# Two-layer image attention: PSUM as four double pairs, keys and queries by pairs of strips, earlier value windows, half of the next image behind layer 0

## The chip, the core and the metric

One core of a Trainium2 chip runs the whole program. Its engines work side by side and meet through semaphores: TensorE (PE; its weight loads are shown as PEld) multiplies into PSUM, VectorE (DVE) and ScalarE (ACT) read PSUM and write SBUF, GpSimd (POOL) works in SBUF alone, and SyncE (SP) issues the DMAs. Each engine takes its own instructions in program order. The metric is the time of one execution on the device in microseconds (us), lower is better; the program runs once over a batch of 16 images.

## What is computed

Each image has 64 x 64 positions and 256 channels in fp32. Two layers follow each other, each a group norm, an attention and a residual add. Layer 0 is linear attention over the whole image, layer 1 is attention over a 7 x 7 neighbourhood with a learned positional term; both have 8 heads of 32 channels.

```python
x = x + L0(_gn(x));  x = x + L1(_gn(x))
# L0, per head: n = 4096 positions
q = softmax(q, over 32 channels) * 32**-0.5;  k = softmax(k, over n)
context = einsum('bhdn,bhen->bhde', k, v);  out = einsum('bhde,bhdn->bhen', context, q) @ w_out
# L1, per position and head: the 49 neighbours (zero padded)
scores = einsum('bhwnd,bhwndk->bhwnk', q, unfold(k, 7) + e)     # e: row and column embeddings
out = einsum('bhwndk,bhwnk->bhwnd', unfold(v, 7), softmax(scores))
```

## The kernel before

An image lies as two tiles of 128 channels x 4096 positions (`x[0]`, `x[1]`), cut into 8 strips of 512. The host has ordered the positions in column blocks: strips 1 to 7 are each 8 columns wide over all 64 rows, shifted by three from the padded grid's blocks; strip 0 holds the two edges (5 and 3 columns) and is moved in two pieces (`pieces`, L474). The main loop runs over the images `b`; one image goes through these stages, in program order on every engine:

1. **Layer 0** (`layer0`, L515). For each of 16 pairs of token blocks PE makes queries and keys (L531) into a two-bank PSUM tile, ACT takes the exponential, and PE adds up the context (L549). `xn[0]` and `xn[1]` hold the normalised image; after the last L531 nothing of this layer reads `xn[1]`. Then the output product (L642) runs in 4 x 2 blocks of 64 matmuls; DVE adds each block to `x` (L653, L656) and takes statistics (L465).
2. **Group statistics** for layer 1 (`group_steps`, L257): DVE aggregates, copies the means (L265), PE averages over groups (L268), DVE forms the variance, PE averages again (L277), POOL makes the reciprocal root (L281).
3. **Positions** (`positional_products` L692, `positional` L703): products of four pairs of strips into four PSUM banks, moved by DVE (pairs 0, 2) and ACT (pairs 1, 3). `fold_bias` (L670) and the `foldv` product (L1036) fold the group means into biases; `bvn` (L1039) is the value bias. `store_rings` (L714) writes the positional scores to DRAM in 16 DMAs.
4. **Values** (`values`, L734): eight strips in the order `KEYED = (2,3,4,5,6,7,1,0)`, 16 matmuls each, a bias add by DVE in two halves (L746), then a DMA to the padded value image `vpad` in DRAM (eight DMAs for strip 0). After the fourth strip `load_rings(0)` (L726) issues eight DMAs that bring positional scores and a mask into rows of `qq`.
5. For each half `hg` of the heads (0, 1): **keys and queries** (`keys_queries`, L760), then **attention** (`local_attention`, L807).

`keys_queries` makes all keys in four steps of two strips, then all queries in four steps. `banks` (L375) hands out PSUM in turn: double tile 0 (moved by DVE), double tile 1 (moved by ACT), single banks 0 and 1, single banks 2 and 3 (one bank by DVE, one by ACT). `evacuate` (L681) moves 32 rows x 512 positions at a time and adds the bias, one instruction for each head and strip (L684 on ACT, L686 on DVE). The last query step is held back by a `yield` until the first scores are issued.

`local_attention` first writes a mask value into both double tiles (L951), then works on four units of 16 columns, in the order `UNITS = (1,2,3,0)`. A unit has nine row chunks in five groups. For each chunk: scores (L834) into a double tile, an exponential on ACT (L843 for half 0, L846 for half 1), weighted values (L878) into single banks 0 and 1 (`outs`, opened by L885), an in-place add of overlapping rows on DVE (L863), and sums (L908) into banks 2 and 3 (`zs`). A step of the loop issues the scores of one group, the weighted values of the group before, the sums of the one before that. At a unit's end ACT copies `outs` (L970), DVE transposes `zs` (L915) and spreads the reciprocals (L921), POOL multiplies and adds to the image (L934, L942), and SP stores finished strips. `vw` holds the value windows of a unit: `load_window` (L795) issues four DMAs from `vpad`, two windows at a time are in SBUF.

Between groups, `between0` and `between1` put in work for the next image: in attention 0 the load of `x_next[1]` strip by strip during units 0 and 1 (L1074) and its statistics during units 2 and 3; in attention 1 the load of `x_next[0]` at the first group, its statistics at unit 1 (two strips per group), the three group-statistics steps at unit 2, groups 0 to 2, and the normalisation (L285) of two strips at unit 3, groups 1 and 2. The storage of `x_next[1]` is the present image's `xn[1]`. The order of PE, ACT, DVE and SP is exactly that of the program text; a DMA's issue on SP waits for what its data need and for the DMA eight issues earlier.

Of the kernel before, what the change touches and what calls it, by code (L numbers as in the profile page):

```python
# [19 lines left out]
P = 128  # L20
W = 64
# [21 lines left out]
ORDER = (4, 5, 6, 7, 0, 1, 2, 3)  # L43
EDGE = (5, 3)
# [44 lines left out]
class Net:  # L89
# [167 lines left out]
    def group_steps(self, stats, eps, small, psum, name, result):  # L257
# [5 lines left out]
        mean_c, var_c = mv[:, :, 0:1], mv[:, :, 1:2]  # L263
        rhs = small.tile([P, 2, 1], F32, tag="gn1", name=f"gn1{name}")
        nc.vector.tensor_copy(rhs, mean_c)  # L265
        yield
        pm = psum(f"pm{name}")
        nc.tensor.matmul(pm[:, 0:2], self.grp, rhs.rearrange("p a b -> p (a b)"), start=True, stop=True)  # L268
# [3 lines left out]
        nc.vector.tensor_tensor(d, rhs.rearrange("p a b -> p (a b)"), mean, ALU.subtract)  # L272
        nc.vector.tensor_tensor(d, d, d, ALU.mult)
        nc.vector.tensor_tensor(d, d, var_c.rearrange("p a b -> p (a b)"), ALU.add)
# [83 lines left out]
def attention_fast(tc, io, ok):  # L358
# [3 lines left out]
    with ExitStack() as ctx:  # L362
# [3 lines left out]
        double = [ps.tile([P, 2, 512], F32, tag=f"pd{i}", name=f"pd{i}") for i in range(2)]  # L366
        single = [ps.tile([P, 512], F32, tag=f"ps{i}", name=f"ps{i}") for i in range(4)]
        turn = [0, 0]

        def psum2():  # L370
            turn[0] += 1
            return double[turn[0] % 2]

        def banks():

            i = turn[1] % 4
            turn[1] += 1
            if i >= 2:
                return single[2 * i - 4 : 2 * i - 2], (0, 1)
            return [double[i][:, j] for j in range(2)], (i, i)  # L380
# [4 lines left out]
        def next_bank(name):  # L385

            return double[(turn[0] + 1) % 2][:, 0, 64:]
# [127 lines left out]
        def layer0(b, x, xn, mean, rstd, xtok, ready, midway=None):  # L515

            mu = None
            pc, other = single[:2], single[2:]
# [92 lines left out]
            for hg in range(2):  # L611
                for h in range(4):
                    rows = slice(HD * h, HD * h + HD)
                    nc.tensor.matmul(
                        double[h // 2][:, h % 2, hg * C : (hg + 1) * C],
                        ch[rows, hg * P : (hg + 1) * P],
                        n.wout_sb[rows, hg],
                        start=True,
                        stop=True,
                    )  # L620
# [3 lines left out]
            for h in range(2):  # L624
                nc.vector.tensor_copy(w4[:, h].rearrange("p g c -> p (g c)"), double[0][:, h])
            nc.scalar.copy(w4[:, 2:4].rearrange("p h g c -> p h (g c)"), double[1])
# [5 lines left out]
            for i in range(NS // 2):  # L632
# [3 lines left out]
                for co in range(2):  # L636
                    py = [double[a // 2][:, a % 2, : 2 * P] if co else single[a][:, : 2 * P] for a in range(4)]
                    for h in range(4):
                        for hg in range(2):
                            for a in range(4):  # L640
                                rows = slice(HD * a, HD * a + HD)
                                nc.tensor.matmul(  # L642
                                    py[a],
# [6 lines left out]
                    if co:  # L650
                        for a in (0, 2):
                            part = double[a // 2][:, :, : 2 * P].rearrange("p a (t n) -> p a t n", n=HD)
                            nc.vector.tensor_tensor(xv[:, a : a + 2], part, xv[:, a : a + 2], ALU.add)  # L653
                    else:
                        for a in range(4):
                            nc.vector.tensor_tensor(xv[:, a], py[a].rearrange("p (t n) -> p t n", n=HD), xv[:, a], ALU.add)  # L656
# [35 lines left out]
        def positional_products(i, x, pair):  # L692
            for k in range(2):
                for a in range(2):
                    nc.tensor.matmul(  # L695
                        single[i][64 * a : 64 * a + 64],
# [6 lines left out]
        def positional(i, pair):  # L703


            for a in range(2):
                for hg in range(2):
                    rows = slice(64 * a + 32 * hg, 64 * a + 32 * hg + 32)
                    image = placed(qq[32 * hg : 32 * hg + 32, 0], hg)
                    for _, _, m, w, view in pieces(pair[a]):  # L710
                        src = view(single[i][rows])
# [22 lines left out]
        def values(b, s, x):  # L734

            pv, _ = banks()
            v4 = work_tile(f"v4_{b}_{s}").rearrange("p (t c) -> p t c", c=C)
            for i in range(2):
                pi = pv[i].rearrange("p (t c) -> p t c", c=C)
                for t in range(2):  # L740
                    n0 = s * 512 + (2 * i + t) * P
                    for k in range(2):
                        nc.tensor.matmul(pi[:, t], x[k][:, n0 : n0 + P], wv[:, k], start=(k == 0), stop=(k == 1))  # L743
            for i in range(2):
                pi = pv[i].rearrange("p (t c) -> p t c", c=C)
                nc.vector.tensor_tensor(v4[:, 2 * i : 2 * i + 2], pi, bv.unsqueeze(1).to_broadcast([P, 2, C]), ALU.add)  # L746
# [13 lines left out]
        def keys_queries(b, hg, x):  # L760

            for what in range(2):
                for i in range(0, NS, 2):
                    if what and i == NS - 2:
                        yield
                    ps, engines = banks()
                    pair = KEYED[i : i + 2]
                    wgt = wq if what else wk
                    for a in range(2):
                        for k in range(2):  # L770
                            nc.tensor.matmul(  # L771
                                ps[a],
                                wgt[:, k, hg * P : (hg + 1) * P],
                                x[k][:, strip(pair[a])],
                                start=(k == 0),
                                stop=(k == 1),
                            )
                    for a in range(2):
                        for h in range(4):
                            rows = slice(h * HD, (h + 1) * HD)  # L780
                            d0 = 64 * (h % 2)
                            for u, p0, m, w, view in pieces(pair[a]):
                                src = view(ps[a][rows])
                                if what:
                                    dst = placed(qq[d0 : d0 + HD, h // 2], hg)[:, :, w : w + m]
                                else:
                                    dst = kaug[h // 2][d0 : d0 + HD, u, PAD : PAD + W, p0 : p0 + m]
                                dst = by_rows(dst, src)
                                if what and hg:

                                    order = "p r w -> p w r" if len(src.shape) == 3 else "p g r w -> p w g r"
                                    dst, src = dst.rearrange(order), src.rearrange(order)
                                evacuate(engines[a], dst, src, bias[rows, 2 * what + hg : 2 * what + hg + 1])
# [13 lines left out]
        def local_attention(b, hg, x, y, vw, queries, after_scores, between, stored):  # L807
# [3 lines left out]
            outs, zs = single[:2], single[2:]  # L811
# [98 lines left out]
            def finish(i, t, r, pvs):  # L910

                for k in range(2):


                    nc.vector.transpose(r[:, k], zs[k])  # L915
# [32 lines left out]
            for i in range(4):  # L948
                rows = slice(32 * i, 32 * i + 32)
                to = double[i // 2][:, i % 2]  # L950
# [3 lines left out]
            for step in range(len(groups) + 4):  # L954
# [8 lines left out]
                if held:  # L963
# [3 lines left out]
                    if g == 4:  # L967
                        rs[i] = [tail.tile([P, 2, 512], F32, tag=f"tail{k}", name=f"r{b}_{hg}_{i}_{k}") for k in range(2)]
                        for j in range(2):
                            nc.scalar.copy(rs[i][1][:, j], outs[j])  # L970
# [23 lines left out]
        with tc.manual_schedule(engines=ORDERED):  # L994
# [23 lines left out]
            for b in range(B):  # L1018
# [3 lines left out]
                load_weights(wk, "wk")  # L1022
                mean, rstd = n.group_stats(st, 1e-5, small, bank, f"1_{b}")
                scale(wpos, n.wpos, rstd)
                pairs = [ORDER[i : i + 2] for i in range(0, NS, 2)]
                positional_products(0, x, pairs[0])
                pb = bank("fold")
                fold_bias(mean, wpos, (4,), pb)
                scale(wv, wv, rstd)
                for i in range(4):  # L1030
                    if i < 3:
                        positional_products(i + 1, x, pairs[i + 1])
# [458 lines left out]
```

## Time and profile before

| | |
|---|---|
| three runs, us | 5888.22 (median), 5876.85, 5892.97 |
| the profiled execution, us | 5892.37, of it 5890.5 in the span |
| busy share of the span | PE 89%, PEld 61%, DVE 58%, ACT 37%, POOL 23% |
| mean granted PE clock | 0.954 |
| DMA | 540.80 MB, 44.1% of 16 engines' time for the program's queue |

The profile is of one execution. "Busy" is the union of an engine's instruction times; matmuls are pipelined, so busy PE is not PE at its peak. A bracket such as [2.35 <-ACT qq L684] behind a row gives the idle time of that engine before the row and what ended it. In the chain of work that ended last, every step is followed back to what released it; "issue" is time in which an engine waited for nothing that the profile shows. A line such as "L684 ACT ACTIVATE qq<-pd,bias 32x512 x8" reads: source line, engine, operation, output and inputs by tile name (pd are the double PSUM tiles, ps the single banks), partitions x elements, and how many instructions in a row were merged.

### The profile page before, as it was taken

The numbers are of one execution on the slowest core, as the hardware profiler recorded it, in microseconds if no ns is written. First come the engines' busy times: TensorE is split into PE (matmuls) and PEld (weight loads), VectorE is DVE, ScalarE is ACT, GpSimd is POOL, SyncE is SP. The second block draws the span as 40 slices with busy tenths as digits, with TensorE's granted clock in tenths as the row PEclk, the third lists the DMA queues.
The fourth block names the chain that finished last, engine by engine and source line by source line (L and its number), as shares of the span: only waits on it lengthen the run. The fifth ranks groups of instructions, "written<-read, shape, count | busy, mean of one in ns | idle before, by whom it ended". The sixth has DMA issues, their size and how long they took to land.

```text
span 5890.5 us, 169110 instructions
## 1 busy us (share of the span) xinstructions
PE 5235.4 (89%) x75313; PEld 3609.8 (61%) x75313; DVE 3439.0 (58%) x5946; ACT 2193.7 (37%) x3089; POOL 1335.2 (23%) x1946
## 2 busy tenths in 40 slices
PE   7889898898998989989889998988989989899997
PEld 4656566566665666656656666565665666656665
DVE  4565655656565565655655556565574655656555
ACT  1341624425144251442514325144351433514335
POOL 3031231302212022130221302213032130321303
PEclk9999999999999999999999999999999999999999
DMA  4543616445173451734517345173451734517344
GB/s 121 107 102 56 133 54 116 101 74 119 42 130 96 76 115 35 131 94 77 117 33 131 94 77 117 33 133 92 79 119 32 136 86 81 114 35 135 87 77 86
DMA packets 751604, 540.80 MB, mean 92 GB/s; under 512 B 241408, under 2 KB 682368, under 8 KB 748416
## 3 DMA queue, kind: packets, MB, share of 16 engines
q1 hardware_dynamic: 750864, 529.89, 44.1%
q8 instruction: 592, 9.70, 0.7%
q14 instruction: 148, 1.21, 0.1%
HBM read 371.04 MB, written 158.73 MB: 90 GB/s over the span
## 4 chain that ended last, share of the span: by engine, by line
PE 77%; DVE 8%; ACT 5%; issue 5%; DMA 2%; SPq 1%; POOL 1%; DVEq 0%; ACTq 0%; POOLq 0%
PE pd L531 15%; PE pd L834 13%; PE ps L878 8%; PE pd L771 7%; PE ps L549 6%; PE ps L771 5%; ACT qq L684 4%; PE ps L642 4%; PE pd L743 4%; PE pd L642 4%; PE ps L743 4%; PE ps L908 4%; DVE e L863 3%; PE ps L695 2%; DMA vpad<-v 1%
## 5 line engine op out<-in xcount | busy, mean ns | idle before, releaser
L863 DVE TENSOR_TENSOR e<-e,e 128x384 f32<-128x384 f32 x1024 | 732.4, 742 | 773.1 <-PE ps L878 615.2
L834 PE MATMUL pd<-qq,kaug 64*64 64x112 f32 (+4 forms) x27648 | 938.0, 277 | 159.8 <-issue 71.1
L834 PEld LDWEIGHTS pd<-qq,kaug 64*64 64x64 f32 x27648 | 813.2, 139 | 319.5 <-issue 181.8
L531 PE MATMUL pd<-wqkv,img 128*128 128x512 f32 x2048 | 948.8, 608 | 3.2 <-DVE img L285 3.2
L443 POOL TENSOR_TENSOR others<-others,rc 128x32 f32<-128x32 f32 x128 | 32.1, 251 | 2858.6 <-DVE rc L919 2858.4
L535 ACT ACTIVATE eq<-pd 128x1024 f32<-128x1024 f32 x256 | 261.9, 1023 | 1077.7 <-PE pd L531 1077.7
L531 PEld LDWEIGHTS pd<-wqkv,img 128*128 128x128 f32 x2048 | 399.1, 196 | 412.1 <-issue 376.6
L878 PE MATMUL ps<-e,vw 128*32 128x112 f32 (+1 forms) x18432 | 575.2, 261 | 65.2 <-issue 64.5
L538 DVE TENSOR_REDUCE qz<-eq 128x16 f32<-128x512 f32 x256 | 175.5, 686 | 766.9 <-ACT eq L535 766.9
L846 ACT ACTIVATE e<-pd 128x896 f32<-128x896 f32 (+2 forms) x576 | 461.4, 836 | 430.5 <-PE pd L834 423.5
L843 ACT ACTIVATE e<-pd 128x896 f32<-128x896 f32 (+2 forms) x576 | 462.4, 838 | 400.7 <-PE pd L834 395.8
L684 ACT ACTIVATE qq<-ps,bias 32x512 f32<-32x512 f32 (+2 forms) x512 | 318.6, 648 | 733.5 <-PE ps L695 668.6
L908 PE MATMUL ps<-e,ones 128*32 128x128 f32 (+2 forms) x10240 | 404.2, 266 | 146.3 <-DVE e L863 113.0
L878 PEld LDWEIGHTS ps<-e,vw 128*32 128x32 f32 x18432 | 419.0, 114 | 154.4 <-issue 117.5
L942 POOL TENSOR_TENSOR img<-img,r 128x320 f32<-128x320 f32 (+1 forms) x512 | 493.2, 993 | 0.0
L549 PE MATMUL ps<-xtok,eq 128*128 128x257 f32 x2048 | 483.4, 380 | 0.0
L549 PEld LDWEIGHTS ps<-xtok,eq 128*128 128x128 f32 x2048 | 387.4, 190 | 149.8 <-issue 107.1
L684 ACT ACTIVATE kaug<-pd,bias 32x512 f32<-32x512 f32 x256 | 173.7, 678 | 674.8 <-PE pd L771 671.9
L686 DVE TENSOR_SCALAR qq<-ps,bias 32x512 f32<-32x512 f32 (+2 forms) x416 | 312.3, 759 | 151.0 <-PE ps L771 145.2
L934 POOL TENSOR_TENSOR r<-r,r 128x512 f32<-128x512 f32 x256 | 340.7, 1352 | 140.5 <-DVE r L921 134.8
L908 PEld LDWEIGHTS ps<-e,ones 128*32 128x32 f32 x10240 | 253.3, 116 | 189.6 <-DVE e L863 148.1
L465 DVE BATCH_NORM_STATS2 st<-img 128x6 f32<-128x512 f32 x512 | 332.1, 679 | 9.7 <-DMA img<-in_xc 5.2
(128 smaller groups left out, 6609.9 us busy)
## 6 DMA issues: line engine op xcount, KB each, us to landing
vw<-vpad SPq DMA_DIRECT2D x512, 288.0 KB
img<-in_xc SPq DMA_DIRECT2D x256, 256.0 KB
xtok<-in_xt SPq DMA_DIRECT2D x64, 1024.0 KB
out<-img SPq DMA_DIRECT2D x256, 256.0 KB
vpad<-v SPq DMA_DIRECT2D x112, 512.0 KB
qq<-pos SPq DMA_DIRECT2D x128, 256.0 KB
qq<-in_ring SPq DMA_DIRECT2D x128, 256.0 KB
pos<-qq SPq DMA_DIRECT2D x128, 112.0 KB
```

Source lines behind the costliest of these rows:

```text
L531: nc.tensor.matmul(ps[:, t], xn[k][:, n0 : n0 + P], n.wqkv_sb[:, k, : 2 * C], start=(k == 0), stop=(k == 1))
L549: nc.tensor.matmul(pc[hg][:, : C + 1], eq[p][:, t, C + hg * P : C + (hg + 1) * P], xtok[p // 4][:, 2 * (p % 4) + t], start=(p == 0 and t = ...
L642: nc.tensor.matmul(py[a], w4[rows, h, hg, co * P : (co + 1) * P], qv[rows, 4 * hg + h, 8 * HD * i : 8 * HD * (i + 1)], start=(h == 0 and h ...
L684: nc.scalar.activation(dst, src, AF.Identity, bias=bias)
L743: nc.tensor.matmul(pi[:, t], x[k][:, n0 : n0 + P], wv[:, k], start=(k == 0), stop=(k == 1))
L771: nc.tensor.matmul(ps[a], wgt[:, k, hg * P : (hg + 1) * P], x[k][:, strip(pair[a])], start=(k == 0), stop=(k == 1),)
L834: nc.tensor.matmul(to, kaug[pl][rows, u, 8 * c : 8 * c + 8].rearrange("p r w -> p (r w)"), q, start=True, stop=True,)
L843: nc.scalar.activation(e.rearrange("p (a n) -> p a n", a=2), ps[:, :, : 2 * m], AF.Exp)
L863: nc.vector.tensor_tensor(part, part, rows_of(c - 1, before, r0, 8 * c), ALU.add)
L878: nc.tensor.matmul(dst, stationary, pr, **flags)
L908: nc.tensor.matmul(dst, ones, pr, start=True, stop=True)
L942: nc.gpsimd.tensor_tensor(yv, xv, by_rows(add[:, :, a - w0 : e - w0], xv), ALU.add)
```

## The change

PSUM's eight banks become four two-bank tiles (`pairs`) used alike by all stages; the single and double tiles and `banks` are gone. Positions use bank 0 of the four pairs, the folds bank 1 of pairs 2 and 1 (and bank 0 of pair 1 after the values); context, `outs` and weighted sums use pairs 2 and 3; scores and the co=1 output blocks use pairs 0 and 1. A value strip is moved by one DVE instruction of 1024 per partition, the `outs` copy and the `zs` transpose are one instruction each. Keys and queries alternate by pairs of strips; where neither strip is strip 0, one instruction moves both strips of a head. Keys go to DVE, queries to ACT; the last query step is divided by heads. The value windows of units 1 and 2 are loaded between the value stores. `x_next[1]` is loaded as a whole after layer 0's code. The means are read where they lie, without a copy. In attention 1 the statistics take one strip per group from unit 0, group 3, the group-statistics steps come at unit 2, groups 1 to 3, and the normalisation one half-strip per group at unit 3.

```diff
+QUERIED = ((0, 1), (2, 3), (4, 5), (6, 7))
...
-        rhs = small.tile([P, 2, 1], F32, tag="gn1", name=f"gn1{name}")
-        nc.vector.tensor_copy(rhs, mean_c)
...
-        double = [ps.tile([P, 2, 512], F32, tag=f"pd{i}", name=f"pd{i}") for i in range(2)]
-        single = [ps.tile([P, 512], F32, tag=f"ps{i}", name=f"ps{i}") for i in range(4)]
+        pairs = [ps.tile([P, 2, 512], F32, tag=f"pair{i}", name=f"pair{i}") for i in range(4)]
...
-            pc, other = single[:2], single[2:]
+            pc, other = ([pairs[i][:, j] for j in range(2)] for i in (2, 3))
...
-                    py = [double[a // 2][:, a % 2, : 2 * P] if co else single[a][:, : 2 * P] for a in range(4)]
+                    py = [pairs[2 - 2 * co + a][:, :, : 2 * P] for a in range(2)]
...
         def values(b, s, x):
-            pv, _ = banks()
+            pv = pairs[KEYED.index(s) % 4].rearrange("p i (t c) -> p (i t) c", c=C)
...
+            nc.vector.tensor_tensor(v4, pv, bv.unsqueeze(1).to_broadcast([P, 4, C]), ALU.add)
...
         def keys_queries(b, hg, x):
+            for i in range(8):
+                pair, what = QUERIED[i // 2], i % 2
+                wgt = wq if what else wk
+                ps = pairs[i % 4]
+                if i == 7:
+                    yield
...
+                for h in range(4):
+                    rows = slice(h * HD, (h + 1) * HD)
...
+                    engine = h // 2 if i == 7 else i % 2
+                    b0 = bias[rows, 2 * what + hg : 2 * what + hg + 1]
+                    if pair[0]:
...
+                        src = ps[rows]
...
+                        evacuate(engine, dst, src, b0)
+                        continue
...
-                for k in range(2):
-                    nc.vector.transpose(r[:, k], zs[k])
+                nc.vector.transpose(r, pairs[3])
...
-                        for j in range(2):
-                            nc.scalar.copy(rs[i][1][:, j], outs[j])
+                        nc.scalar.copy(rs[i][1], pairs[2])
...
                 load_weights(wk, "wk")
+                if more:
+                    x_next, xn_next = halves(b + 1)
+                    load_half(b + 1, 1)
...
-                pb = bank("fold")
+                pb = pairs[2][:, 1]
...
-                pv = bank("foldv")
+                pv = pairs[1][:, 1]
...
                     if i == 3:
                         load_rings(0)
+                    if i in (5, 6):
+                        vw[i - 5] = load_window(b, 0, UNITS[i - 5])
-                pb = bank("fold2")
+                pb = pairs[1][:, 0]
...
-                vw = {i: load_window(b, 0, UNITS[i]) for i in range(2)}
...
-                    if more and g < 4:
-                        s = ORDER[4 * (i % 2) + g]
-                        if i < 2:
-                            nc.sync.dma_start(x_next[1][:, strip(s)], xc[b + 1, :, 1, strip(s)])
-                        else:
-                            strip_stats(st, x_next, 1, s)
+                    if more and i >= 2 and g < 4:
+                        strip_stats(st, x_next, 1, ORDER[4 * (i % 2) + g])
...
-                    if i == 1 and g < 4:
-                        for s in ORDER[2 * g : 2 * g + 2]:
-                            strip_stats(st, x_next, 0, s)
-                    if i == 2 and g == 0:
+                    at = 5 * i + g - 3
+                    if 0 <= at < NS:
+                        strip_stats(st, x_next, 0, ORDER[at])
+                    if at == NS:
                         steps = n.group_steps(st, 1e-5, small, next_bank, f"0_{b + 1}", gn)
-                    if i == 2 and g < 3:
+                    if NS <= at < NS + 3:
                         next(steps, None)
-                    if i == 3 and g in (1, 2):
-                        normalise(xn_next, x_next, *gn, ORDER[g - 1])
+                    if i == 3 and g < 4:
+                        k, o = g % 2, strip(ORDER[g // 2])
+                        n.normalise(xn_next[k][:, o], x_next[k][:, o], *gn, k)
```

## The prediction

> **What bounds it now.** I read the page first: engine shares, then the chain that ended last. TensorE (PE) is busy 89% of the span and carries 77% of the chain, so a microsecond is won only where PE waits or is slowed.
>
> ```profile
> PE 5235.4 (89%) x75313; PEld 3609.8 (61%) x75313; DVE 3439.0 (58%) x5946; ACT 2193.7 (37%) x3089; POOL 1335.2 (23%) x1946
> PE 77%; DVE 8%; ACT 5%; issue 5%; DMA 2%; SPq 1%; POOL 1%; DVEq 0%; ACTq 0%; POOLq 0%
> ```
>
> Next I cut one image (2954.84 to 3325.50 us) at the first matmul of each kind and asked for the windows view: length, busy time of PE, PEld, DVE, ACT, POOL, granted clock, DMA share, GB/s. The rows are layer 0, its output product, positions, values, keys/queries and attention of half 0, the same of half 1.
>
> ```profile
> 2954.84:3045.45 90.61, 87.84 (x315) 51.12 (x311) 39.32 (x93) 17.06 (x17) 30.97 (x60) 0.98 0.14 46
> 3045.45:3079.89 34.44, 28.88 (x516) 26.95 (x517) 23.43 (x51) 0.33 (x1) 0.70 (x1) 0.96 0.01 2
> 3079.89:3092.73 12.84, 10.38 (x44) 4.02 (x44) 8.65 (x15) 6.79 (x8) 0.00 (x0) 0.84 0.01 1
> 3092.73:3123.74 31.01, 30.74 (x160) 26.56 (x160) 11.70 (x21) 0.71 (x1) 0.00 (x0) 0.94 0.90 150
> 3123.74:3151.04 27.30, 24.95 (x64) 10.75 (x61) 21.09 (x29) 17.86 (x29) 0.00 (x0) 1.00 1.09 196
> 3151.04:3223.04 72.00, 60.39 (x1779) 48.13 (x1777) 39.02 (x59) 37.50 (x54) 21.61 (x24) 0.93 0.44 101
> 3223.04:3249.83 26.79, 24.94 (x64) 10.74 (x61) 24.18 (x34) 18.42 (x31) 5.93 (x9) 1.00 1.18 139
> 3249.83:3325.50 75.67, 64.33 (x1782) 52.05 (x1780) 47.88 (x72) 38.29 (x56) 23.68 (x27) 0.85 0.38 106
> ```
>
> Over all 16 images the same cuts average 91.15, 35.86, 11.70, 29.54, 27.34, 68.94, 27.45 and 74.62 us: 366.6 each, times 16 plus 25.0 before the first image gives the span, 5890.5. The loss sits in the two attentions and at the seams into them; DMA is full (1.09, 1.18) over keys/queries and empty (0.01) over the output product. The PE timeline of the seam, with the idle time before a row in brackets:
>
> ```profile
> 3150.72 0.39 PE L951 MATMUL pd<-bits,nb 32*128 32x512 bf16 x2 [2.35 <-ACT qq L684]
> 3151.04 1.58 PE L834 MATMUL pd<-qq,kaug 64*64 64x64 f32 x48
> 3152.55 5.21 PE L771 MATMUL ps<-img,wqn 128*128 128x512 f32 x8
> 3157.69 1.56 PE L834 MATMUL pd<-qq,kaug 64*64 64x112 f32 x48
> ...
> 3162.24 2.74 PE L834 MATMUL pd<-qq,kaug 64*64 64x112 f32 x48 [1.92 <-ACT e L843]
> ```
>
> Two waits for ScalarE, and behind each the same work runs slower (5.21 us where eight such matmuls took 3.60 just before, at 3144.45; 2.74 for 1.56). ScalarE's timeline shows why:
>
> ```profile
> 3144.65 6.02 ACT L684 ACTIVATE qq<-pd,bias 32x512 f32<-32x512 f32 x8 [1.94 <-PE pd L771]
> 3157.80 3.45 ACT L684 ACTIVATE qq<-ps,bias 32x320 f32<-32x320 f32 x8 [2.67 <-PE ps L771]
> ```
>
> It gets a whole query pair in eight instructions while PE needs the pair's banks next, and later eight more ahead of the exponentials.
>
> [...] The clock records agree on the length (545.6 us at 0.5, in multiples of 3.41 us), but a window need not be wholly idle: of 104 drops the median window before had PE idle 62%, and 65 windows with over 40% idle stayed at full clock. So a 1.9 us gap can cost a slow window (1.7 us)[...]. [...] Here queue q8 moved 9.70 MB in 592 packets[...]. PE's "issue" gaps (167.1 us for L834, L878, L908) fall where the engines are full: 1.33 and 1.39 us right after the window load of 3173 (DMA share 1.04 in 3174 to 3182). [...] For N=512 [...] the trace has 747 and 678 to 710[...].
>
> **The change, part by part, per image.**
>
> Instruction size. An evacuation of 1024 in place of two of 512: DVE [...] 1.28 us (two took 1.52), ACT [...] 1.14 (two: 1.38 to 1.5); strided query writes may make ACT 1.3, I take 1.2 (1.1 to 1.4). Two banks in one read cost nothing extra: L653 reads two banks at 686 ns per 512 elements, L746 one at 687.
>
> Keys/queries. PE does a strip pair in 3.45 us, order k01 q01 k23 q23 k45 q45 k67 | q67; keys go to DVE, queries to ACT. From the stage's start S: DVE has k01 in 4 x (0.65+0.46+0.75) = 7.5 at most, S+3.5 to 11.0, k23 to 16.1, k45 from 17.3 to 22.5. ACT has q45 from S+20.8 to 25.6. PE is at the masking matmuls L951 at S+24.6 and waits for ACT 1.0 in place of 2.35 (half 0), about 0.9 for 1.85 (half 1): -1.35, -0.95; I book -1.2 and -0.95. Then q67 is split, two instructions each, ACT S+31.1 to 33.5, and the exponential that frees the third scores' bank ends at 34.4, PE comes at 33.7: waits 0.7 for 1.92 and 1.80: -1.2, -1.2. [...] The clock records have 3.06 and 2.52 us at half clock in the first 16 us of the two attentions, half of it lost: of 2.8 I book -2.0. DVE has k67 out at S+29.5; L885 needs its banks at S+32.6.
>
> Positions and values. foldv now uses pair 1, values start on pair 0: the wait of L743 for L1039 (17.2 us, 8 times, 1.1 per image) goes. But foldv shares a tile with position pair 1, whose ScalarE evacuation ends some 0.5 us after PE's products (3085.8 + 4 x 0.95 against 3089.1), and in the built program foldv does wait for ScalarE; behind it on PE stand the value matmuls: -0.6 net. A value evacuation of 1024 takes 1.25 instead of 0.69 after the last matmul; the second half of fold2 waits for a DVE step queued behind it, with the key matmuls next on PE: +0.65 (0.27 now). Other values are covered by 3.45 us of matmuls per strip.
>
> Group statistics. One DVE copy (0.17, L265) less on the path behind the output product: -0.2. In attention 1 the steps move one group later, off the unit whose GpSimd work slows DVE (L863 pair 2.08 where it takes 1.03; copy 0.91 for 0.17): PE waits there 2.2 per image and the middle of attention 1 has 6.5 us at half clock. Bounds -0.5 and -3.5, I take -1.5. The tail: four normalisations spread over four groups, one of 0.7 falls behind the last sum: -0.7.
>
> Loads. Eight 256 KB DMAs leave attention 0's SP queue and stand behind wk's load, waiting for layer 0's last reads (up to 3036); next in SP's queue are the position stores, 56 us later (3092.3). The cover is the empty output product; without it the 2 MB are about 9 us of DMA (238 GB/s over 3257 to 3267, where the other half is loaded). Gain: the last image has neither these loads nor the statistics; its attention 0 takes 63.5 against 69.3 for the other 15, so 5.8 is the roof, 1 the floor (window loads keep saturating DMA): -2.5. In SP's queue the four window loads of unit 1 pass the nine stores of strips 1 and 0, the four of unit 2 the last eight. Strip 0's stores are then issued until about 3145 in place of 3137.6 (the eight loads took 7.64 us of issue); waiting on them are the unit 3 window (3173) and the fifth and sixth exponential, which reuse their buffers (about 3163): covered by 12 us. Windows were no wait before: nothing won.
>
> Output adds (4 of 256 to 2 of 512: 1.42 to 1.29 us), tail copies and transposes of both banks at once: hidden under PE's 3.45 us per block and 1.56 us of scores; uncovered 0.5 us each at most.
>
> Sum: -0.2 -0.6 +0.65 -2.15 -2.4 -2.0 -1.5 -0.7 -2.5 = -11.4 us, times 16 = 182, less 4.7 that the last image can't gain: 178. From the profiled run's 5892.4 (2 us around the span) that is 5714; the median runs lie 0.07% below: 5710. With every term at its low end (loads 1, statistics 0.5, no tail, clock 1.0, ACT at 1.4) it is about 4.6 per image (5815), at the high ends (loads 5, statistics 3.5, clock 2.8) about 16.5 (5630).
>
> **Rivals.** (a) Partial: fetch gaps and half-clock windows, which move with every shift, fall elsewhere as often; only seam waits go: about 5 to 6 per image, 5795 to 5810. For it: the same stage varies between images, attention 1 from 70.2 to 78.1 in the first 15 with the same work. (b) Nothing shows: what is won is refilled by fetch gaps[...]: 5880 to 5900. Against: DMA share in attention 0 falls by 2 of about 7 MB. (c) Slower: evacuation becomes the bound. All keys are DVE's, 7.5 + 3 x 4 x d + 2 d per half in 26 us. PE waits from d = 1.7 us (k45 before the masking matmuls); a half then runs 8d - 15.7 us longer than now, plus 4d - 8 over d = 2 for k67, and what is won elsewhere (4.9) is gone at d = 2.2; at 2.5, 6010. Against: L653's 686 ns[...].
>
> **Numbers.** Main case (5650 to 5775) 0.58, more than that 0.06, (a) up to 5870 0.24, (b) 0.04, (c) 0.08. A change below 0.3% (18 us) can't be told from none here. Range 5630 to 5830: it leaves out (b), (c), the end of (a) and a little below.
>
> **What would show it.** Right: L951's wait near 1.0; the wait for the third scores under 1; keys/queries near 26.0; keys 1.25 to 1.35 on DVE per 1024; attention 0 near 62 to 65; no image load between 3147 and 3200 of such an image; DMA over 0.2 in layer 0's second half or its output product; foldv waiting for ACT 0.5. Wrong: query evacuations over 1.4 us, waits on window or value stores in attention 0, "issue" gaps in the output product, or half-clock time not under 480 us.

## The result

The changed kernel takes 5905.04 us (median of 20 runs, 5875.18 to 5927.79) where the kernel before takes 5880.22 us on the same chips (20 runs): a ratio of 1.0031, 95% interval 1.0017 to 1.0046. That is 25 us slower, 0.3%. The prediction was 5710 us (5630 to 5830), so it has the wrong sign and misses by 195 us.

The page of the changed kernel, engine shares:

```profile
PE 5244.2 (89%) x75313; PEld 3611.0 (61%) x75313; DVE 3418.4 (58%) x5338; ACT 2002.1 (34%) x2385; POOL 1357.3 (23%) x1946
```

PE is busy 9 us more than before for the same 75313 matmuls, though ACT has 704 instructions less and DVE 608 less. The clock records fit a PE that is busy longer: 595.7 us at half clock, where the kernel before had 545.6.

The windows view of one image, cut as in the prediction (layer 0, output product, positions, values, keys/queries and attention of half 0, the same of half 1; columns as there):

```profile
2968.56:3059.74 91.18, 87.92 (x315) 51.26 (x311) 39.87 (x92) 17.07 (x17) 31.02 (x60) 0.98 0.21 70
3059.74:3093.98 34.24, 28.88 (x517) 26.94 (x517) 22.75 (x42) 0.32 (x1) 0.70 (x1) 0.96 0.01 2
3093.98:3104.80 10.82, 10.36 (x45) 4.25 (x46) 6.73 (x13) 4.75 (x6) 0.00 (x0) 0.81 0.00 0
3104.80:3134.55 29.75, 28.95 (x162) 25.27 (x160) 12.85 (x16) 2.78 (x3) 0.00 (x0) 1.00 1.00 165
3134.55:3162.48 27.93, 26.64 (x64) 11.33 (x61) 18.45 (x23) 15.79 (x20) 0.00 (x0) 0.94 0.97 195
3162.48:3232.81 70.33, 57.52 (x1779) 45.99 (x1777) 42.35 (x57) 34.13 (x42) 21.64 (x24) 0.96 0.33 69
3232.81:3261.17 28.36, 27.56 (x64) 11.71 (x61) 20.93 (x27) 15.37 (x21) 5.87 (x8) 0.91 1.17 149
3261.17:3333.45 72.28, 59.72 (x1782) 47.98 (x1780) 49.01 (x68) 34.84 (x42) 23.71 (x27) 0.93 0.37 103
```

The image loads did move: DMA share in layer 0 is 0.21 (0.14 before), in attention 0 0.33 (0.44). Attention 0 is still 70 us. PE's timeline at the seam of this image:

```profile
3162.16 0.39 PE L945 MATMUL pair<-bits,nb 32*128 32x512 bf16 x2 [1.29 <-ACT qq L670]
3162.48 1.36 PE L829 MATMUL pair<-qq,kaug 64*64 64x64 f32 x48
3163.77 3.70 PE L752 MATMUL pair<-img,wqn 128*128 128x512 f32 x8
3167.40 1.56 PE L829 MATMUL pair<-qq,kaug 64*64 64x112 f32 x48
3168.89 0.39 PE L880 MATMUL pair<-bits,nb 64*128 64x512 bf16 x2
3169.21 0.81 PE L873 MATMUL pair<-e,vw 128*32 128x64 f32 x32
3173.69 2.89 PE L829 MATMUL pair<-qq,kaug 64*64 64x112 f32 x48 [3.66 <-ACT e L838]
```

The wait at the masking matmuls is 1.29 for 2.35, close to the 1.0 of the forecast. But the third scores wait 3.66 us for the exponential, where they waited 1.92 before and were to wait 0.7. That gap fills nearly all of the 3.41 us before 3173.27, from where the clock records have half clock for 3.41 us, and the next scores run slower (2.89 us where 1.56 is usual). ScalarE's timeline, then VectorE's:

```profile
3157.15 4.96 ACT L670 ACTIVATE qq<-pair,bias 32x1024 f32<-32x1024 f32 x4 [1.84 <-PE pair L752]
3163.29 1.53 ACT L838 ACTIVATE e<-pair 128x512 f32<-128x512 f32 x2 [1.18 <-issue]
3170.22 2.47 ACT L670 ACTIVATE qq<-pair,bias 32x1024 f32<-32x1024 f32 x2 [5.41 <-DVE qq L672]
3172.72 1.73 ACT L838 ACTIVATE e<-pair 128x896 f32<-128x896 f32 x2
```

```profile
3160.59 5.16 DVE L672 TENSOR_SCALAR kaug<-pair,bias 32x1024 f32<-32x1024 f32 x4 [1.70 <-PE pair L752]
3167.56 2.57 DVE L672 TENSOR_SCALAR qq<-pair,bias 32x1024 f32<-32x1024 f32 x2 [1.82 <-issue]
```

Here is the fault. The last query pair is ready at 3167.4. VectorE starts on its two heads without delay and is done at 3170.13. ScalarE is idle and has two heads of the same pair to move, yet begins at 3170.22, and what it waited for is VectorE. Behind its two stands the exponential that frees the bank of the third scores. The waits of ScalarE's evacuation line, summed over the run (waited for, us, times), show that this is so in every one of the 32 halves:

```profile
L670 ACT ACTIVATE qq<-pair,bias x832: 384/743/1410, 174.4 to 5827.8; 32x1024 f32<-32x1024 f32 x64, 32x512 f32<-32x512 f32 x52, 32x192 f32<-32x192 f32 x26, 32x320 f32<-32x320 f32 x25
...
  DVE qq L672: 172.8, 32
```

ScalarE is done with the pair 5.24 us after PE's last query matmul in half 0 (5.00 in half 1), where before it was done after 3.48 (3.37). The waits grew by as much: 1.86 and 1.65. Per image, all 16 averaged, in us:

| | before | changed |
|---|---|---|
| layer 0 | 91.15 | 92.02 |
| output product | 35.86 | 35.98 |
| positions | 11.70 | 11.16 |
| values | 29.54 | 29.75 |
| keys/queries 0 | 27.34 | 26.77 |
| attention 0 | 68.94 | 70.19 |
| keys/queries 1 | 27.45 | 27.01 |
| attention 1 | 74.62 | 74.55 |
| sum | 366.6 | 367.4 |
| PE waits for masking banks, halves 0 and 1 | 2.35, 1.85 | 1.21, 0.80 |
| PE waits for the exponential, 0 and 1 | 1.91, 1.80 | 3.77, 3.45 |
| half clock in the first 16 us of attention 0, 1 | 3.06, 2.52 | 5.26, 4.58 |

### The profile page after: what moved, and what is told of

It reads as the page before. It is cut to its first block, busy times and chain, and to the rows that moved or that the text cites. A ratio compares the mean times of both kernels' runs of the same rounds, so it can differ in the third digit from the quotient of the medians.

```text
span 5903.7 us, 168064 instructions
## 1 busy us (share of the span) xinstructions
PE 5244.2 (89%) x75313; PEld 3611.0 (61%) x75313; DVE 3418.4 (58%) x5338; ACT 2002.1 (34%) x2385; POOL 1357.3 (23%) x1946
## 5 line engine op out<-in xcount | busy, mean ns | idle before, releaser
L670 ACT ACTIVATE qq<-pair,bias 32x1024 f32<-32x1024 f32 (+3 forms) x832 | 680.0, 847 | 1642.0 <-PE pair L681 671.5
L829 PE MATMUL pair<-qq,kaug 64*64 64x112 f32 (+4 forms) x27648 | 939.2, 278 | 202.3 <-issue 62.8
L829 PEld LDWEIGHTS pair<-qq,kaug 64*64 64x64 f32 x27648 | 817.4, 139 | 358.5 <-issue 175.0
L521 PE MATMUL pair<-wqkv,img 128*128 128x512 f32 x2048 | 950.9, 610 | 6.2 <-DVE img L284 6.2
L672 DVE TENSOR_SCALAR kaug<-pair,bias 32x1024 f32<-32x1024 f32 (+3 forms) x768 | 689.0, 922 | 225.4 <-PE pair L752 219.8
L525 ACT ACTIVATE eq<-pair 128x1024 f32<-128x1024 f32 x256 | 262.2, 1024 | 1072.1 <-PE pair L521 1072.1
L873 PE MATMUL pair<-e,vw 128*32 128x112 f32 (+1 forms) x18432 | 567.7, 260 | 53.8 <-issue 53.4
L841 ACT ACTIVATE e<-pair 128x896 f32<-128x896 f32 (+2 forms) x576 | 463.7, 835 | 434.3 <-PE pair L829 427.1
L838 ACT ACTIVATE e<-pair 128x896 f32<-128x896 f32 (+2 forms) x576 | 464.4, 836 | 404.3 <-PE pair L829 333.6
L752 PE MATMUL pair<-img,w 128*128 128x512 f32 x1024 | 492.4, 626 | 0.0
L539 PE MATMUL pair<-xtok,eq 128*128 128x257 f32 x2048 | 483.4, 380 | 0.0
L752 PE MATMUL pair<-img,wqn 128*128 128x512 f32 x1024 | 463.6, 595 | 0.0
```

Of the source, the lines that this page charges most:

```text
L521: nc.tensor.matmul(ps[:, t], xn[k][:, n0 : n0 + P], n.wqkv_sb[:, k, : 2 * C], start=(k == 0), stop=(k == 1))
L539: nc.tensor.matmul(pc[hg][:, : C + 1], eq[p][:, t, C + hg * P : C + (hg + 1) * P], xtok[p // 4][:, 2 * (p % 4) + t], start=(p == 0 and t = ...
L670: nc.scalar.activation(dst, src, AF.Identity, bias=bias)
L672: nc.vector.tensor_scalar(dst, src, bias, None, ALU.add)
L752: nc.tensor.matmul(ps[:, a], wgt[:, k, hg * P : (hg + 1) * P], x[k][:, strip(pair[a])], start=(k == 0), stop=(k == 1),)
L829: nc.tensor.matmul(to, kaug[pl][rows, u, 8 * c : 8 * c + 8].rearrange("p r w -> p (r w)"), q, start=True, stop=True,)
```

## The experiments

**Theory 1: the shared tile.** Two engines that evacuate one PSUM pair take turns, so that splitting the last query pair makes ScalarE late instead of early. More generally, merging banks into one tile merges the waits on them. **Theory 2: refill.** Whatever is won at one wait comes back as fetch gaps (TensorE waiting for its next instructions, the "issue" gaps) and half-clock windows. Two terms of the prediction, the loads and the statistics, are tested by themselves. Each kernel is compared with the kernel before on the same chip; across groups of runs, ratios are compared.

### The last query pair on VectorE alone (q_dve)

```diff
-                    engine = h // 2 if i == 7 else i % 2
+                    engine = 0 if i == 7 else i % 2
```

> The changed kernel, with all four evacuations of the last query pair on VectorE (two are ScalarE's in it). Theory 1, the shared tile: in the changed kernel ScalarE's two wait until VectorE's two are done (they start 2.76 us after TensorE's last query matmul, end at 5.24, where the kernel before ended at 3.48), so the exponential that frees the third scores' bank is late: 3.77 and 3.45 us of waiting per image. Here ScalarE is free at once: those two waits fall under 0.7 us each (-6 per image), the half-clock time in the first 16 us of the attentions falls from 5.26 and 4.58 us towards 3 (-2 per image at half loss), VectorE's longer queue (5.2 us) gives back up to 1: -7 per image, 5790 us (5750 to 5830). Theory 2, refill: what is won at this wait comes back as instruction-fetch gaps and half-clock windows: within 30 us of the changed kernel, 5875 to 5925.

Measured 5780.16 us, before 5887.17 there: ratio 0.9805 (0.9776 to 0.9834). One line turns the loss of 0.3% into a gain of about 2%. PE at the seam of the same image, then ScalarE:

```profile
3118.57 1.56 PE L829 MATMUL pair<-qq,kaug 64*64 64x112 f32 x48
3120.07 0.39 PE L880 MATMUL pair<-bits,nb 64*128 64x512 bf16 x2
3120.39 0.81 PE L873 MATMUL pair<-e,vw 128*32 128x64 f32 x32
3121.13 1.56 PE L829 MATMUL pair<-qq,kaug 64*64 64x112 f32 x48
3122.63 0.97 PE L873 MATMUL pair<-e,vw 128*32 128x112 f32 x32
3123.96 0.27 PE L903 MATMUL pair<-e,ones 128*32 128x32 f32 x8 [0.36 <-DVE qq L672]
```

```profile
3114.42 1.56 ACT L838 ACTIVATE e<-pair 128x512 f32<-128x512 f32 x2 [1.14 <-issue]
3119.60 1.73 ACT L838 ACTIVATE e<-pair 128x896 f32<-128x896 f32 x2 [3.62 <-PE pair L829]
```

The third scores wait for nothing and run at full speed; ScalarE now waits for PE. VectorE is done 5.26 us after the last query matmul, and all that this costs is 0.36 us at the first sums. Over all images the waits for the exponential fall to 0.11 in half 0 and none in half 1, the half-clock time in the first 16 us of both attentions to 0.0, the whole run's to 454.0 us. Theory 1 holds in size (5790 expected). Theory 2 is right in part: these rows alone are worth 10.4 us per image (7.1 of waits, 4.0 as the estimated half of the 7.9 us in which PE worked at half clock, less 0.7 of new waits at the first sums), and the eight stages sum to 7.3 less (367.4 to 360.1). Attention 1 has 0.7 more of issue gaps and 0.5 more of waits for VectorE's sums.

### The last query pair on ScalarE alone (q_act)

```diff
-                    engine = h // 2 if i == 7 else i % 2
+                    engine = i % 2
```

> The changed kernel, with all four evacuations of the last query pair on ScalarE. Theory 1 (the two engines take turns on one tile, so the split wins nothing): ScalarE is done 4 x 1.24 = 5.0 us after the last query matmul, where it is done at 5.24 now: the waits for the exponential stay at 3.4 to 3.8 us and the time is that of the changed kernel within 20 us. If the split does help and ScalarE is late for another reason, the four instructions come on top of that: the exponential 2.5 us later in each half, +5 per image, 5985 us.

Measured 5891.17 us, ratio 1.0003 (0.9987 to 1.0019). ScalarE at the seam:

```profile
3150.98 4.98 ACT L670 ACTIVATE qq<-pair,bias 32x1024 f32<-32x1024 f32 x4 [2.71 <-PE pair L752]
3155.98 1.73 ACT L838 ACTIVATE e<-pair 128x896 f32<-128x896 f32 x2
```

Four instructions on one engine end 5.01 us after the last query matmul; two and two on both engines ended at 5.24. The split wins nothing, and the waits for the exponential are much like those of the changed kernel (3.51 and 2.93 per image). By the ratios the time is 0.3% under that of the changed kernel, within the 20 us of the first forecast and far from the 5985 of the second.

### Another order of the pairs (d_seq)

```diff
-                ps = pairs[i % 4]
+                ps = pairs[(0, 3, 2, 1, 0, 3, 2, 3)[i]]
```

on top of q_dve.

> q_dve, and the eight strip pairs of keys and queries use the double banks in the order 0,3,2,1,0,3,2,3 in place of 0,1,2,3,0,1,2,3, so that neither of the two that the masking matmuls write still waits for ScalarE's third query pair. Theory 1: the wait at the masking matmuls (1.21 and 0.80 us per image) goes too, and nothing takes its place, since the third query pair's bank is next needed 4 us later: q_dve less 2 per image, -32 us, 5758. Theory 2: no different from q_dve within 15 us.

Measured 5755.55 us, ratio 0.9763 (0.9734 to 0.9792), on the chip of q_dve (5780.16): 25 us, of 32 expected. Keys/queries lose their waits wholly (1.29 and 0.79 per image, now none). Inside the attentions 0.79 and 0.29 us come back, inside the first scores: they read the third query pair itself, and ScalarE is not done with it when TensorE comes that much earlier. These gaps of up to 0.79 us left the first 16 us of the attentions without half clock.

### The bias foldings before the last value strip (d_seqfold)

On top of d_seq:

```diff
-                pb = pairs[1][:, 0]
-                fold_bias(mean, wk, (0, 1), pb)
-                fold_bias(mean, wq, (2, 3), pb)
...
+                    if i == 6:
+                        fold_bias(mean, wk, (0, 1), pairs[0][:, 0])
+                        fold_bias(mean, wq, (2, 3), pairs[1][:, 0])
```

> d_seq, and the two bias foldings of keys and queries stand before the last value strip, each in a pair of its own (0 and 1), in place of behind it in one pair. Theory 1 (each wait on one shared tile is paid on TensorE): the wait of 0.80 us per image at the second folding goes, and the slow first key pair behind it (5.40 us in place of 3.60 in part of the images: the clock records have 1.49 us per image at half clock in keys/queries of half 0) with it: -1.3 per image, d_seq less 20, 5735 us. Theory 2 (refill): d_seq within 10 us.

Measured 5724.09 us, ratio 0.9736 (0.9721 to 0.9752), 0.27% under the last one's ratio; the intervals overlap, but the rows are plain. The 0.80 us wait is gone, the value stage falls from 29.75 to 28.87 us in every image, and keys/queries 0 has no half-clock time left (1.49 us per image before this edit). PE was idle in only 23% of the 3.41 us ahead of each of those seven drops; another 1.24 us of them went to the 32 one-column matmuls of the foldings, which the profile counts as busy. The same matmuls without the wait (d_seqfold) bring no drop.

### The context product in another pair (f_ct)

On top of d_seqfold:

```diff
-                            other[1][rows, hg * P : (hg + 1) * P].rearrange("p (a d) -> p a d", a=4),
+                            pairs[0][rows, 1, hg * P : (hg + 1) * P].rearrange("p (a d) -> p a d", a=4),
...
-            nc.vector.tensor_scalar(ch, other[1][:, :C], SCALE, None, ALU.mult)
+            nc.vector.tensor_scalar(ch, pairs[0][:, 1, :C], SCALE, None, ALU.mult)
```

> d_seqfold, and in layer 0 the product of context and value weights is written to pair 0 in place of the second bank of pair 3, whose first bank VectorE is still reading. Theory 1 (a wait goes by the pair as one tile, not by its banks): the wait before that product, 1.00 us per image in the changed kernel and 0.60 before, falls back to 0.60, all else alike: -0.4 per image, 6 us, about what the time can tell; 5718 us. Rival: the wait stays at 1.0, since it is for the data.

Measured 5710.22 us, ratio 0.9707 (0.9684 to 0.9731); this is the fastest kernel of the study. The row that decides is who waited for VectorE's line L588, which reads bank 0 of the pair (us, times): first the kernel without this edit, then with it.

```profile
  PEld pair L593: 19.8, 16
  PE pair L593: 15.9, 16
```

```profile
  PEld pair L593: 17.2, 32
  PE pair L593: 9.7, 16
```

15.9 us over 16 images is 1.00 each, 9.7 is 0.60, the value of the kernel before (9.7 us too). The product used to go to bank 1 of a pair whose bank 0 VectorE still read: another bank, and TensorE waited for both of VectorE's reads. Now it starts behind the first. So in this program a wait goes by the pair as a whole. The time fell by about 0.3% against the last kernel's ratio (the intervals overlap at their ends), more than the 6 us of the wait; half-clock time in layer 0 and the output product fell from 5.12 + 5.19 to 3.85 + 2.77 us per image. Its place points to this wait, which stands at the end of layer 0: in the last 12 us of layer 0 and the first 12 of the output product PE had 1.74 + 2.10 us per image at half clock without the edit, and none with it in any of the 16 images (nor in f_loads, the same kernel but for its loads), while the other waits there are the same. The kernel before had 0.31 + 0.56 there, the changed one 1.74 + 1.88.

### The loads (b_loads, d_loads, f_loads)

Moved alone, in the kernel before (b_loads):

```diff
                 load_weights(wk, "wk")
+                if more:
+                    x_next, xn_next = halves(b + 1)
+                    load_half(b + 1, 1)
...
-                        if i < 2:
-                            nc.sync.dma_start(x_next[1][:, strip(s)], xc[b + 1, :, 1, strip(s)])
...
```

> The kernel before, with one part of the change alone: the eight loads of half 1 of the next image are issued behind layer 0 in place of inside attention 0. The prediction's term: -2.5 us per image of 15, 5880 - 37 = 5843 us, with issue gaps of attention 0 down from 6.2 to about 4.9 us. Rival (the window loads saturate the DMA anyway, and fetch gaps fall elsewhere): within 12 us of 5880.

Measured 5858.73 us, ratio 0.9945 (0.9922 to 0.9967): 28 us by the medians. The interval allows 19 to 46 us, so the 37 of the prediction are not excluded. Attention 0's issue gaps fall from 6.23 to 5.18 us per image, its half-clock time from 7.52 to 5.56. Taken back in q_dve (d_loads):

> q_dve, with the eight image loads in attention 0 again, as in the kernel before. The prediction's term is 2.5 us per image of 15 (+37), the move alone in the kernel before won 28: 5808 to 5817 us, with attention 0's issue gaps up from 4.75 to about 6 us. Rival (the gaps that the loads cause were only paid because attention 0 already stood): within 10 us of q_dve.

Measured 5780.96 us, ratio 0.9841 (0.9826 to 0.9855); 0.9805 with the move, intervals overlapping, issue gaps 6.57 for 4.75. Taken back in the fastest kernel, f_ct, on the same chip as that one:

> f_ct with the eight image loads in attention 0 again. The prediction's term for their move behind layer 0 is 2.5 us per image of 15 (37 us), the move alone in the kernel before won 28: here 5718 + 28 to 37 = 5746 to 5755 us, with attention 0's issue gaps about 1.5 us per image up. Rival (the gaps are paid only where attention stands anyway): within 10 us of f_ct.

Measured 5724.80 us, ratio 0.9730 (0.9707 to 0.9752): 15 us, neither the 28 to 37 nor plainly nothing; the intervals overlap by half. Issue gaps are 6.07 for 4.75. In all three the gaps move by 1.0 to 1.8 us per image, and the time by 1 to 2 us per image by the medians and ratios, not 2.5. That the issue gaps are waits for instructions can be read from the traces: in the kernel before, all 124 of them in the attentions (167.0 us) end 1.2 to 1.8 us after a 16 KiB packet of the instruction queue q8 has ended, a place in which only 11% of the time in these stages lies.

### The statistics (b_stats, d_stats)

The placing of the change alone, in the kernel before (the last four hunks of the diff):

> The kernel before with the change's placing of statistics, group steps and normalisations in attention 1 alone. The prediction's terms, 1.5 + 0.7 per image of 15: 5880 - 33 = 5847 us. By the stages of the changed kernel, where the waits for the mean and for the sums fell by 0.3 and 0.7 per image together: 5880 - 15 = 5865 us, and less if ScalarE's or the fetch's waits take it.

Measured 5876.46 us, ratio 1.0001 (0.9984 to 1.0018): nothing, give or take 10 us. And the old placing, in q_dve:

> q_dve, with statistics and normalisations of attention 1 placed as in the kernel before (two strips' statistics in each of four groups of the second unit, the group steps in the third, normalisations two at a time). The prediction's terms: 1.5 + 0.7 us per image back, q_dve + 33, 5813 us. Rival, by the stages of the changed kernel (wait for the statistics' mean 1.23 us per image where it was 1.31, attention 1's waits for VectorE's sums 4.5 to 5.0 where they were 5.2): the move wins next to nothing, within 12 us of q_dve, 5768 to 5792.

Measured 5781.44 us, ratio 0.9846 (0.9824 to 0.9868). Against 0.9805 that is 0.4% slower, give or take about as much, so this run decides little by itself: once the seam is empty, the new placing may be worth something. Its rows have the waits for the mean and variance at 1.50 and 0.65 us per image for 1.21 and 0.24, the sums' waits for VectorE at 5.88 for 4.96, and issue gaps at 3.70 for 4.62: a microsecond moves from one wait to the other.

### The early windows (d_win)

```diff
-                    if i in (5, 6):
-                        vw[i - 5] = load_window(b, 0, UNITS[i - 5])
...
+                vw = {i: load_window(b, 0, UNITS[i]) for i in range(2)}
```

in q_dve.

> q_dve, with the window loads of the first two units behind the value stores again, as in the kernel before. The prediction booked nothing for their move: within 10 us of q_dve, 5770 to 5790. Rival (windows early take DMA time from the value stores and delay the third unit's window, or keep TensorE's instruction fetch waiting): faster by 15 us or more without the move.

Measured 5771.19 us, ratio 0.9821 (0.9805 to 0.9838): not to be told from 0.9805. The early windows neither won nor lost anything that these runs resolve.

### The cure without the change (b_dve)

In the kernel before, the last query pair on VectorE alone:

```diff
                     ps, engines = banks()
+                    if what and i == NS - 2:
+                        engines = (0, 0)
```

> The kernel before with one edit of its own: the last query pair's evacuations all on VectorE (it has the second strip's eight on ScalarE, done 3.48 us after the last query matmul). Theory 1 (what counts at this seam is that ScalarE is free for the exponentials, whatever the rest of the change does): its two waits for the exponential, 1.91 and 1.80 us per image, fall under 0.4 each (-3), and the half-clock time in the first 16 us of the attentions, 3.06 and 2.52 us, goes too (half of it: -2.8); VectorE's longer queue gives back up to 0.5: -5.3 per image, 5795 us (5780 to 5820). Rival: the waits of the kernel before are short enough to be refilled, within 20 us of 5880.

Measured 5825.73 us, ratio 0.9909 (0.9886 to 0.9932): 57 us, between the two forecasts. The two waits for the exponential fall to 0.04 and none (-3.7 per image, a little more than expected), but attention 0 keeps 2.59 of 3.06 us at half clock in its first 16 us; attention 1 keeps 0.78 of 2.52. The wait at the masking matmuls is still 2.35 and 1.85, and the sums' waits for VectorE rise from 1.84 to 2.64 in attention 0 and from 5.23 to 6.13 in attention 1, more than the 0.5 that was allowed for. The seam was worth something before the change too, but a free ScalarE alone did not empty it; in the changed kernel it did. Which other part of the change that takes was not run apart.

## Why the prediction was wrong

**The step that failed** is this one: "Then q67 is split, two instructions each, ACT S+31.1 to 33.5". From PE's last query matmul ScalarE was to need 0 to 2.4 us; it needed 2.76 to 5.24. I took two engines on one pair to work side by side, as they had in the kernel before: there VectorE moved the last pair from 1.68 us before PE's end to 1.36 after it and ScalarE from 0.04 to 3.48, both writing `qq` at the same time, but each out of its own single-bank tile. That `qq` can be written by both at once excludes it as the cause. In the trace, ScalarE's first instruction stands behind a semaphore that VectorE's second one sets, and begins 0.1 us after that one's end in all 32 halves; the prediction looked at such waits for the bias products only. The prediction had met the same thing once ("foldv shares a tile with position pair 1", measured 0.49 us per image for 0.5) and did not carry it over.

VectorE's heads here are partitions 0 to 63 and ScalarE's 64 to 127, so the two share no partition of the pair. The 32 waits of 32 (172.8 us), and L593's wait across two banks (15.9 us in 16 waits, 9.7 with the product in another pair), show that this program guards by the tile, not by bank or partition. Whether the chip would have let the two run together, and a split with a tile of its own for each engine, no run here shows.

What this one step was worth: the waits for the exponential were to change by -2.4 us per image and changed by +3.5; the half-clock windows in the first 16 us were to give -2.0 and took +1.2, counted as half of the time (PE worked 7.9 us per image at half clock there, 5.6 before; the rest of their 9.8 us fell into the waits). That is an estimated 9 us per image, 145 us per run, of the 195 missed. Setting the step right won 2.3% (from a ratio of 1.0031 to 0.9805, some 130 us), with both terms then beyond their forecast (-3.6 and -2.8, less 0.7 for the sums).

**The other terms.**

- Masking waits, -1.2 and -0.95: measured -1.06 and -1.05 (the profile puts 0.74 of half 0's old wait and 0.08 of the new one down to a DMA; both are counted in). Right. A key evacuation of 1024 takes 1280 ns on VectorE (forecast 1.28), a query one on ScalarE 1169 on average, up to 1.24 (forecast 1.2). Both forecasts were the author's estimates: the kernel before moves keys and queries by 512 at most, out of the double tiles in 747 ns on VectorE and 678 to 710 on ScalarE. Keys/queries take 26.8 and 27.0 us, not 26.0, since half-clock time in them rose from 0.14 and 1.35 to 1.07 and 2.56.
- Positions -0.6: -0.54. Right. Second folding +0.65: the wait grew from 0.39 to 0.80; half-clock time behind it was not in the sum. The copy of the means, -0.2: the wait ahead of the mean's product fell from 3.40 to 3.20 us per image. Right.
- Statistics -1.5 and tail -0.7: 0, by the run of their own in the kernel before (b_stats). The waits did fall in the changed kernel's attention 1 (mean and variance from 1.31 + 0.50 to 1.23 + 0.24, sums 5.23 to 4.48), but the time did not follow. Probably the error was to count a wait of 2.2 us in one unit as won when its work moved to another unit of the same attention; this was not tested.
- Loads -2.5: 1 to 2 by the medians, up to 3.1 by the interval of b_loads. Right in direction, probably too large. The "roof" was taken from the last image, which lacks the statistics too.
- Clock: in the kernel before, half clock comes in stretches of 3.41 us and multiples of it, and in the 3.41 us ahead of its 104 drops PE was idle for 38% and more (median 62%, over 40% in 102 of them). The prediction counts 65 windows that stayed at full clock with PE idle over 40%; on one grid laid over the span I find 53. Its reading, that idle time of this size goes with a drop often but not always, stands. But two waits of 0.61 and 0.55 us make up most of those 38%, and in the changed kernel five drops have 23%, with one wait of 0.80 us. The -2.0, booked for gaps of 0.7 and 1.0 us, was an estimate: in these traces the length of a gap alone does not tell whether a drop comes with it.
- Not in the sum at all: L593's wait, +0.4 per image, from the merging of banks 0 and 1 of pair 3, and with it 2.8 us more at half clock around the start of the output product, by estimate another 1.4 lost. The wait for ScalarE's copy L963 rose from 0.10 to 0.73 us in attention 0 and from nothing to 0.42 in attention 1. Ahead of that copy ScalarE waits for GpSimd's last adds (110.2 us over the run, 37.1 before), so the merged copy need not be the reason. In attention 0 this wait goes with the loads: their move alone, in the kernel before, raised it from 0.10 to 0.39, and with them back (d_loads) it is 0.21. By what way stays open.

**The rivals.** The slower one was given 0.08 for another reason: VectorE as the bound, which by the author's estimate begins at 1.7 us per 1024, and 1.28 was measured. None of them had the two engines in a queue. "Partial" and "nothing shows" took the seam waits to be won first.

In the fastest kernel the seam's waits are small (none at the masking matmuls, 0.1 us for the exponential, 0.79 and 0.29 for the third query pair, 0.4 at the first sums) and the images sum to 355.0 us each (366.6 before), with 345.9 us at half clock. That it stands at 5710 us, the number of the forecast, is chance: it has four edits that the change lacks.

## What to carry to other kernels

When single banks are merged into larger tiles, list for each merged tile which engines touch it within one stage: every pair of engines that used to work on different banks side by side may now take turns, and an even split between two engines then ends as late as one engine alone (here 5.24 us after the last query matmul by two, 5.01 by ScalarE alone). Give the last tile before a hand-over wholly to the engine that is not needed next; its longer queue cost 0.7 us of waiting per image here, and the image became 7.3 us shorter. And read the waits of the built program for every split instruction, not only for those that look suspicious.

## What was not expected of the hardware

Half-clock time went with the waits, so that they cost more than their own length. The two waits of 3.77 and 3.45 us per image went with 7.9 us in which PE worked at half clock in the first 16 us of the attentions, by estimate 4 us lost on top of 7.2. With the waits gone, this was 0.0 in all 32 halves; gaps of 0.4 us at the same place left it at 0.0. Small waits can go with it too. At the end of layer 0, when the wait at L593 fell from 1.00 to 0.60 us per image (f_ct), the 3.8 us at half clock there went to nothing. In keys/queries 0 the wait of 0.80 us ahead of the stage and 1.49 us at half clock in it vanished together; the windows before those drops were 77% busy by the profile, but 36% of each were one-column matmuls. So in these traces PE's busy share alone does not tell which windows drop.
